# Moving half of the scores of squares of 16 to GpSimd and the gate's remainders to TensorE and ScalarE, in a four-layer hybrid kernel

## The chip, the cores and the metric

The kernel runs on one core of one Trainium2 chip. The metric is the device time of one execution in microseconds (us). The engines are called by the names that the profile uses: PE (TensorE, matrix products), PEld (its weight loads), DVE (VectorE), ACT (ScalarE), POOL (GpSimd) and SP (SyncE, which only issues transfers here). Each engine runs its own instructions strictly in the order in which they were written, and waits on semaphores for the others.

## The reference

Eight batches of 512 tokens of width 256 go through four residual layers, each on the layer-normed input: attention A, feed-forward, attention B, feed-forward.

```
Q, K, V = heads of x@Wq*C**-0.5, x@Wk, x@Wv     # 16 heads, C = 64
scores  = einsum('bshq,bshk->bshqk', Q, K)      # per token and head: 64 x 64
w       = softmax(scores masked to k <= q)
attn    = einsum('bshqk,bshk->bshq', w, V)
x = x + attn @ Wo                               # attention A

h = silu(x@w1 * s1) * (x@w2 * s2)               # the gate, 1024 wide
h = gelu(h@h1 * s);  h = gelu(h@h2 * s)         # two hidden layers
x = x + (h@w3) * s3                             # feed-forward
```

Attention A isn't attention over tokens. For every token and head it forms the outer product of the 64 query and 64 key entries, takes a causal softmax over it, and weighs the value entries. It has no matrix product in its core, so the work is elementwise, on DVE, ACT and POOL. Attention B is ordinary causal attention over the tokens, with 16 heads of 16.

## The kernel before

**Attention A.** The lower triangle of each 64 x 64 square is cut into squares: one of 32 x 32, two of 16 x 16, four of 8 x 8 and so on for each head, and the diagonal. A group is one tile of 128 tokens and four heads (256 columns); there are 8 x 4 x 4 = 128 groups. The work of a group is split into four units (line 553): unit 0 is the squares of 32 of two heads, unit 1 all squares of 16, unit 2 the squares of 32 of the other two heads, unit 3 the small squares. A unit goes through these stages, some steps apart:

- `scores` (line 784): the products of queries and keys, in pieces of 128 x 1024 elements. Units 0 and 2 run on POOL, two pieces each; units 1 and 3 on DVE, unit 1 in two pieces. POOL takes the query from an SBUF copy, DVE from PSUM.
- `exps` (line 798): the exponential, on ACT.
- `weigh` (line 808): times the values, on DVE.
- `halve` (line 814): one half of a unit's columns is added onto the other by a transfer that POOL issues.
- `fold` (line 819): for the squares of 32, POOL adds the two halves of what is left.
- `gather` (line 845): DVE sums over columns, into a small tile `red`.
- `add_rows` (line 852): POOL adds `red` to the group's accumulator. Then `invert` (line 856, DVE) and `divide` (line 860, POOL).

`AttentionA.step(n)` writes one step: unit n is scored, unit n-1 goes through the exponential, unit n-2 is weighed and halved, units n-3 to n-5 are folded and gathered. A step has three parts, set off by `yield`. The second part begins with the scores of units 1 and 3; then come the adds of the sums that were gathered before, the division, the small squares (lines 835 and 852) and the folds. The tile of unit 1 (`w16`) has one buffer, that of units 0 and 2 three.

**The rest.** Feed-forward and attention B of a batch are written as one generator, `after_a`, and are woven between the parts of attention A's steps. Each `yield` of the generator gives a number; the main loop draws from it until the sum of these numbers reaches `total` times the share of the batch's 64 steps that attention A has done. So the yields and `total` (line 1339) together set how far apart pieces of the feed-forward are written. Work of the other batch lags attention A by 75 steps: attention A runs alone at first, and the last batch's other layers run alone at the end.

**The gate.** Products are taken in fp32r, one pass each, so what comes out of the gate is kept as a high and a low part. For each of the eight chunks of 128 x 512 of a feed-forward: PE makes two products into two PSUM tiles; ACT takes silu of the first (line 1028); DVE multiplies by the second (line 1031); ACT rounds the result to fp32r (line 1035), the high part; POOL subtracts that from the result (line 1036), the low part. Each of these is written with `later`, and `flush` writes what is pending, so every chunk goes one stage further with each flush. The five buffers of PSUM pool `ps_f` rotate over all of this work. `plus` (line 472) adds a tile to a PSUM tile by a product with the identity. The hidden layers' products are line 1120, their gelus lines 1085 and 1087, their weights come by transfers which POOL issues (line 934). The feed-forward's last product is line 1146, attention B's are lines 1167 to 1276.

## Time and profile before

| what | value |
|---|---|
| time of three runs | 4002.61, 4003.38, 4004.08 us, median 4003.38 |
| the profiled execution | 4009.55 us, its span 4007.6 us |
| mean granted clock of PE | 0.845 |
| line 784 on POOL, 128 x 1024 | 512 instructions, mean 2102 ns |
| line 784 on DVE, squares of 16, 128 x 1024 | 256 instructions, mean 1219 ns |
| line 852 on POOL, sums of 32, 128 x 128 | 256 instructions, mean 701 ns |
| line 852 on POOL, sums of 16, 8 and 4, 128 x 256 | 384 instructions, mean 759 ns |
| line 819 on POOL, folds, 128 x 1024 | 256 instructions, mean 2512 ns |
| line 1036 on POOL, the gate's low part, 128 x 512 | 128 instructions, mean 1448 ns |
| line 1035 on ACT, the gate's high part, 128 x 512 | 128 instructions, mean 615 ns |

The profile shows one execution. Its span runs from the first to the last instruction; the execution's own time is a little longer. The mean of a group of instructions includes an overlap: where instructions follow each other without a gap, the distance from start to start is shorter than the mean, by 0.1 to 0.3 us. Busy shares are of the span, and an engine can be busy at its share and still wait for another once in each round.

### The profile page before, as it was taken

Reading aid. Unit: us, or ns where it says so; the run is one execution under the profiler, and the core shown is the slowest. Engines: PE = TensorE matmul, PEld = TensorE weight load, DVE = VectorE, ACT = ScalarE, POOL = GpSimd, SP = SyncE. Lnnn points to the kernel's source line nnn. Section 1 sums busy time; section 2 is a strip of 40 time slices with the busy share of each in tenths; the row PEclk is TensorE's granted clock in tenths of the full one; section 3 lists DMA queues with packets and bytes.
Section 4 is the critical chain, followed back from the end, with each engine's and each line's share of the span. In section 5 each row is a group of like instructions: output and inputs, shape, how many; then the busy total and the mean of one; then the engine's idle time right before and its main releaser. Section 6 shows DMA issues by size and latency. Waiting matters only on the chain.

```text
span 4007.6 us, 37678 instructions
## 1 busy us (share of the span) xinstructions
PE 2958.0 (74%) x12328; PEld 2012.2 (50%) x12328; DVE 3376.7 (84%) x3777; ACT 2337.2 (58%) x3145; POOL 3098.1 (77%) x3051
## 2 busy tenths in 40 slices
PE   1543478777876888768787788768787778768988
PEld 0311145355653656346553566346653556436847
DVE  4899988998889888998989988998889988897115
ACT  2433465666755766666755767567656667555342
POOL 6688888887888887887888888888888878886211
PEclk7555689888987989889897889879898899879999
DMA  8566777668776777668776688668877687767304
GB/s 240 114 141 145 146 182 182 147 161 199 199 162 126 195 188 196 150 147 210 174 192 139 168 198 214 147 131 198 195 181 151 154 199 205 155 133 210 126 29 167
DMA packets 118653, 671.07 MB, mean 167 GB/s; under 512 B 12704, under 2 KB 31915, under 8 KB 43824
## 3 DMA queue, kind: packets, MB, share of 16 engines
q0 software_dynamic: 78336, 570.46, 62.9%
q1 hardware_dynamic: 40112, 98.11, 6.8%
q8 instruction: 100, 1.64, 0.2%
q14 instruction: 105, 0.86, 0.1%
HBM read 255.90 MB, written 9.96 MB: 66 GB/s over the span
## 4 chain that ended last, share of the span: by engine, by line
DVE 38%; PE 16%; POOL 14%; DMA 12%; issue 8%; ACT 8%; POOLq 0%; DVEq 0%; ACTq 0%
DVE red L845 15%; DMA w<-w 12%; DVE w L808 10%; PE ph L1120 5%; ACT w L798 3%; POOL w L819 3%; DVE ws L808 3%; POOL w L784 3%; PE pqkb L1167 3%; DVE ws L784 3%; POOL acc L852 3%; DVE w L784 2%; POOL w L814 2%; DVE acc L856 2%; POOL h L1036 2%
## 5 line engine op out<-in xcount | busy, mean ns | idle before, releaser
L798 ACT ACTIVATE w<-w 128x2048 f32<-128x2048 f32 x384 | 734.2, 1913 | 653.8 <-POOL w L784 440.8
L1120 PE MATMUL ph<-h,hidden 128*128 128x512 f32 x4096 | 1047.9, 412 | 77.4 <-POOL h L1036 45.5
L784 POOL TENSOR_TENSOR w<-k 128x1024 f32<-128x1024 f32 x512 | 1076.2, 2102 | 9.6 <-ACT k L762 9.0
L1120 PEld LDWEIGHTS ph<-h,hidden 128*128 128x128 f32 x4096 | 795.3, 196 | 282.1 <-POOL h L1036 55.9
L808 DVE TENSOR_TENSOR w<-w,qv 128x1024 f32<-128x1024 f32 x768 | 899.8, 1213 | 22.4 <-ACT w L798 22.3
L845 DVE TENSOR_REDUCE red<-w 128x128 f32<-128x1024 f32 (+1 forms) x384 | 601.8, 1567 | 171.6 <-DMA w<-w 94.6
L819 POOL TENSOR_TENSOR w<-w 128x1024 f32<-128x1024 f32 x256 | 643.1, 2512 | 72.5 <-DMA w<-w 71.9
L814 POOL DMA_DIRECT2D w<-w x384 | 337.1, 878 | 339.7 <-issue 134.8
L852 POOL TENSOR_TENSOR acc<-acc,red 128x256 f32<-128x256 f32 (+1 forms) x640 | 471.0, 736 | 152.3 <-DVE red L845 124.5
L845 DVE TENSOR_REDUCE red<-ws 128x256 f32<-128x2048 f32 (+1 forms) x256 | 435.5, 1743 | 0.0
L746 PE MATMUL qv<-wqv,xnta 128*128 128x512 f32 x512 | 299.3, 715 | 89.9 <-DVE ws L808 82.4
L808 DVE TENSOR_TENSOR ws<-ws,qv 128x1024 f32<-128x1024 f32 (+3 forms) x512 | 294.7, 638 | 49.4 <-ACT ws L798 49.4
L1052 PE MATMUL pw<-xnt,gate 128*128 128x512 f32 (+2 forms) x1152 | 298.8, 419 | 24.9 <-ACT silu L1028 18.0
L784 DVE TENSOR_TENSOR w<-qv,k 128x1024 f32<-128x1024 f32 x256 | 301.3, 1219 | 3.6
L784 DVE TENSOR_TENSOR ws<-qv,k 128x1024 f32<-128x1024 f32 (+3 forms) x512 | 299.8, 648 | 0.0
L868 PE MATMUL bank<-ident,acc 128*128 128x128 f32 x256 | 64.3, 341 | 287.5 <-ACT k L761 287.1
L798 ACT ACTIVATE ws<-ws 128x1920 f32<-128x1920 f32 x128 | 231.5, 1809 | 75.3 <-DVE ws L784 74.7
L1052 PEld LDWEIGHTS pw<-xnt,gate 128*128 128x128 f32 x1152 | 227.6, 213 | 82.1 <-ACT silu L1028 22.3
L1229 ACT ACTIVATE eb<-psb 128x256 f32<-128x256 f32 (+3 forms) x512 | 182.2, 443 | 146.6 <-PE psb L1226 146.3
L1146 PE MATMUL pof<-w,h 128*128 128x256 f32 x1024 | 247.9, 396 | 19.4 <-ACT h L1085 19.4
L1085 ACT ACTIVATE h<-ph,s_sb 128x512 fp32r<-128x512 f32 (+1 forms) x256 | 171.1, 688 | 145.9 <-PE ph L1120 144.6
L856 DVE RECIPROCAL acc<-acc 128x256 f32<-128x256 f32 x128 | 223.2, 1744 | 12.3 <-POOL acc L852 12.3
(143 smaller groups left out, 4723.5 us busy)
## 6 DMA issues: line engine op xcount, KB each, us to landing
w<-w POOLq DMA_DIRECT2D x384, 1024.0 KB, 7.7
hidden<-in_h POOLq DMA_DIRECT2D x128, 1024.0 KB, 7.9
gate<-in_w12p POOLq DMA_DIRECT2D x32, 1024.0 KB, 9.0
w<-w_d SPq DMA_DIRECT2D x16, 1024.0 KB, 12.0
wqv<-wqv_d SPq DMA_DIRECT2D x31, 512.0 KB
wo<-in_wo SPq DMA_DIRECT2D x32, 256.0 KB, 7.4
wbqk<-wbqk_d SPq DMA_DIRECT2D x8, 1024.0 KB
w<-in_h SPq DMA_DIRECT2D x8, 1024.0 KB, 7.0
```

The lines of the kernel that those rows point to most:

```text
L746: nc.tensor.matmul(qv.rearrange("p j f -> p (j f)"), xnt[:, c, :], wqv[:, c, :], start=(c == 0), stop=(c == DC - 1),)
L784: eng.tensor_tensor(e, rows(q).to_broadcast(shape), columns(kt[:, 0]).to_broadcast(shape), ALU.mult)
L798: nc.scalar.activation(e, e, AF.Exp, scale=C**-0.5)
L808: nc.vector.tensor_tensor(ev, e, columns(qv[:, 1]).to_broadcast(list(e.shape)), ALU.mult)
L814: nc.gpsimd.dma_start(w[:, :2048], w[:, 2048:], accum_op=ALU.add)
L819: nc.gpsimd.tensor_tensor(w[:, :1024], w[:, :1024], w[:, 1024:2048], ALU.add)
L845: nc.vector.tensor_reduce(red, self.columns_of(w, n, off, nsq), AX.X, ALU.add)
L852: nc.gpsimd.tensor_tensor(rows, rows, part.rearrange("p a (x i) -> p a x i", i=n), ALU.add)
L856: nc.vector.reciprocal(acc[:, 0, :], acc[:, 0, :])
L1052: nc.tensor.matmul(pj[:, toks], w[:, m % 4, j, c, :], xs[:, p, c, toks], start=(p == 0 and c == 0), stop=(p == 1 and c == DC - 1),)
L1120: nc.tensor.matmul(pss[j], w[:, j, c, :], h_in(p, c), start=(p == 0 and c == 0), stop=(p == 1 and c == MC - 1),)
L1146: nc.tensor.matmul(po, h(0, c)[:, i * P : (i + 1) * P], w3[:, c, :], start=(c == 0), stop=False)
```

## The change

Four things are edited, and the pacing is adapted to them.

- Scores: the first of the two pieces of the squares of 16 is computed on POOL; the second stays on DVE. It is written where unit 1 was written before, at the start of the second part of its step.
- Sums of 32: units 0 and 2 write their sums into the two halves of one tile, which has one buffer, and POOL adds both to the accumulator at once, after unit 2. The tiles for 16, 8 and 4 have two buffers in place of three.
- Gate: in place of POOL's subtraction, PE makes the difference in PSUM, by a product of the identity with the result and one of the negative identity (`minus`, a new constant) with the high part, and ACT copies that into the low part. This is one stage more.
- Pacing: the gate flushes after each of its two products, not after both; its yields grow by 1.0 or 1.1 per chunk and there are three closing flushes in place of two; `total` goes from 309.5 to 328.9.

```diff
+    minus = const.tile([P, P], F32R, name="minus")
+    nc.scalar.activation(minus, ident, AF.Copy, scale=-1.0)
...
-            eng, q = (nc.gpsimd, kt[:, 1]) if n_u in (0, 2) else (nc.vector, qv[:, 0])
             for n, off, nsq, cols in squares(units[n_u]):
-                for e, ev, rows, columns in pieces(w, n, off, nsq, cols):
+                for p, (e, ev, rows, columns) in enumerate(pieces(w, n, off, nsq, cols)):
+
+                    on_pool = n == 32 or n == 16 and p == 0
+                    eng, q = (nc.gpsimd, kt[:, 1]) if on_pool else (nc.vector, qv[:, 0])
                     shape = list(e.shape)
                     eng.tensor_tensor(
...
                 if n > 2:
-                    red = ap_.tile([P, 2, nsq * n], F32, tag=f"red{nsq * n}", name=f"red_{b}_{i}_{g}_{n_u}_{n}", bufs=2 + (n < 32))
-                    nc.vector.tensor_reduce(red, self.columns_of(w, n, off, nsq), AX.X, ALU.add)
-                    self.sums.append((b, i, g, n, cols, red))
+                    if n_u != 2:
+                        red = ap_.tile(
+                            [P, 2, GW // 2], F32, tag=f"red{n // 32}", name=f"red{n}_{b}_{i}_{g}", bufs=1 + (n < 32)
+                        )
+                        self.live["red", n] = red
+                    red = self.live["red", n]
+                    part = red[:, :, cols.start // 2 : cols.stop // 2]
+                    nc.vector.tensor_reduce(part, self.columns_of(w, n, off, nsq), AX.X, ALU.add)
+                    if n_u != 0:
+                        self.sums.append((b, i, g, n, slice(0, GW), red))
...
             def high():
                 nc.scalar.copy(h(0, m), x)
-                later(lambda: nc.gpsimd.tensor_tensor(h(1, m), x, h(0, m), ALU.subtract))
+                later(low)
+
+            def low():
+                rest = ps_f.tile([P, S], F32, tag="pf", name=f"rest_{u}_{m}")
+                nc.tensor.matmul(rest, ident, x, start=True, stop=False)
+                nc.tensor.matmul(rest, minus, h(0, m), start=False, stop=True)
+                later(lambda: nc.scalar.copy(h(1, m), rest))
...
                 for j in range(2):
                     products(p[j], m, j, last if ps[0] else slice(0, S))
-                flush()
+                    flush()
                 later(lambda m=m, p=p, h=h: gate(m, *p, h))
-                yield 0.5 if ps[0] else 1.8
-        for _ in range(2):
+                yield 1.5 if ps[0] else 2.9
+        for _ in range(3):
             flush()
             yield 1
...
-    total = 309.5
+    total = 328.9
```

## The prediction

> **What bounds the kernel now.** I read the busy shares of the engines first, then the same shares by stretch of the span, then the timelines of GpSimd and VectorE in one quiet stretch, then the table of waits.
>
> ```profile
> PE 2958.0 (74%) x12328; PEld 2012.2 (50%) x12328; DVE 3376.7 (84%) x3777; ACT 2337.2 (58%) x3145; POOL 3098.1 (77%) x3051
> ```
>
> ```profile
> 200.00:600.00 400.00, 191.47 (x464) 107.26 (x463) 386.09 (x412) 181.55 (x197) 347.05 (x320) 0.62 0.71 153
> ...
> 1800.00:2200.00 400.00, 317.33 (x1359) 215.24 (x1359) 358.83 (x392) 257.33 (x345) 330.93 (x317) 0.89 0.76 180
> ...
> 3700.00:3800.00 100.00, 97.72 (x430) 80.63 (x429) 13.86 (x22) 33.68 (x57) 20.09 (x33) 0.98 0.40 132
> ```
>
> The columns of a stretch are its ends and length, then busy time of PE, weight loads, DVE, ACT and POOL. There are three regimes. Up to the first silu at 532 us the first attention runs alone and DVE is busy 386 of 400 us. From there to 3690 us feed-forward and second attention run between its steps, and DVE falls to 359 of 400 with POOL at 331: neither is full. In the last 317 us PE alone is busy.
>
> In the quiet regime a group (four units, one pass over 256 columns) takes 23.72 us: the chain of waits has its three reductions at 153.65, 177.37, 201.09 us and so on. One group on POOL, then on DVE (start, length, [idle before]):
>
> ```profile
> 255.77 0.87 POOL L814 DMA_DIRECT2D w<-w  x1 [2.66 <-issue]
> 256.38 2.35 POOL L852 TENSOR_TENSOR acc<-acc,red 128x128 f32<-128x128 f32 x3
> ...
> 263.79 2.62 POOL L819 TENSOR_TENSOR w<-w 128x1024 f32<-128x1024 f32 x1
> 266.29 0.81 POOL L852 TENSOR_TENSOR acc<-acc,red 128x256 f32<-128x256 f32 x1
> ...
> 269.36 2.36 POOL L819 TENSOR_TENSOR w<-w 128x1024 f32<-128x1024 f32 x1
> 271.68 1.95 POOL L784 TENSOR_TENSOR w<-k 128x1024 f32<-128x1024 f32 x1
> ...
> 263.86 2.28 DVE L845 TENSOR_REDUCE red<-w 128x256 f32<-128x2048 f32 x1
> 266.18 2.36 DVE L784 TENSOR_TENSOR w<-qv,k 128x1024 f32<-128x1024 f32 x2
> ...
> 272.17 1.22 DVE L845 TENSOR_REDUCE red<-w 128x128 f32<-128x1024 f32 x1
> ```
>
> DVE never stops. POOL's only pause is 2.66 us, before it issues the halving transfer of the squares of 16 (line 814), which waits for DVE's weighing. From there POOL runs without a gap to the second fold (line 819), which ends at about 271.70, and DVE needs that fold at 272.17. So POOL is 0.47 us from setting the pace, whatever its share of 77% says. The loop through both engines is: transfer issue to end of fold on POOL, 271.70 - 255.77 = 15.93; the reductions and the weighing on DVE up to the next issue, 1.13 + 3.32 + 2.26 = 6.71 by start-to-start times; 0.6 for two handovers (weighing ends 255.23, issue 255.77). That is 23.25, beside DVE's own 23.72.
>
> ```profile
> DVE silu L1031 <- ACT silu L1028: 55.0, 28, 5.0
> ...
> PE ph L1120 <- POOL h L1036: 45.5, 26, 6.0
> ...
> ACT silu L1028 <- POOL h L1036: 43.0, 30, 3.5
> ```
>
> The columns are total us, times and longest. These waits are the gate's: POOL's subtraction (line 1036) holds the next silu, and that holds DVE and PE.
>
> **What the Trainium skill says.** "GPSIMD Engine Reference", section 3.1, has two-input elementwise work about 1.96 times slower on GpSimd than on VectorE; here the same 1024 elements of line 784 take 2102 ns against 1219, a ratio of 1.72. "Perfetto Trace Analysis", section Identifying the Most-Contended Engine, would have the fullest engine relieved first; that engine is DVE, and the change does it, but the loop above is one that shares of busy time don't show. "PSUM — Partial Sum Buffer" says that GpSimd cannot touch PSUM; the code agrees, for the POOL piece takes its query from the SBUF copy kt[:, 1].
>
> **The change part by part.**
>
> *Squares of 16.* DVE loses one of two pieces a group: 266.18 + 2.36 for two, start to start 2.27, so 1.13 each. POOL gains one piece at 1.92 (start to start, from 250.46 to 252.38; the nearest rows bound it: DVE's own 1.13, and 2.32 for POOL's fold of the same size, which would make the loop 0.4 longer, some 25 us over the kernel's tight groups). It stands in the second part of step 1, ahead of the add of the previous group's sums of 16, the small squares and the second fold. Its tile w16 has one buffer, so it waits for DVE's reduction of the previous group, which ends at 266.14; POOL comes free at 266.29, so the wait costs nothing now. But everything queued behind is 1.92 late, the second fold first; DVE's reduction of it waits, and behind that on DVE stand 3.32 us of reductions and the weighing that the next transfer waits for. The exponential of this unit has 6 us of room (ends 270.53, used at about 276.6), so it isn't late.
>
> *Sums of 32.* Two adds of 128x128 become one of 128x256 at about the same price (rows of 701 and 759 ns), so one of 0.73 goes from POOL. It stood at 252.38, straight before the 2.66 us pause, so the loop gains nothing; if the pause were gone it would be worth 0.73 x 128 = 93 us. The DVE reductions stay. The buffers (one for 32, two for the rest) are written 6 or more us after the adds that free them: nothing.
>
> Quiet regime: DVE alone would need 23.72 - 1.13 = 22.59; the loop needs 23.25 + 1.92 = 25.17. Period up by 1.45. From 142 to 532 us there are 390 / 23.72 = 16.4 groups: **+24 us**.
>
> *The same in the middle regime.* For each of its 109 groups I took from the timeline by how much DVE arrives after the second fold's end. If the room is r, the change is 1.92 - r, but not below -1.13. By classes: 37 groups with r near 0.49 (most of second attention): +53. 26 with r about 1.72: +5. 20 with r over 2.2 (mean 5.2, around the gates): -23. 9 where DVE already waits for POOL's fold: +17. 17 where the fold itself waits some 4 us for its transfer, in which the new piece is hidden: at best -1.13 or a little less, -14 together. Sum **+38 us**. PE also works harder per step here, as the pacing total goes from 309.5 to 328.9, so other stages pass in 6% fewer steps; the -23 and -14 may not be had, so this term is +35 to +75.
>
> *Gate.* Off POOL: 128 subtractions, 1.3 us each start to start, 166 us in all, some 8 in each of 16 stages. On PE: an fp32 identity product of 512 columns and an fp32r one. The tail gives 16 fp32 products of 256 columns in 3.45 us, so 0.43 for 512; and 256 fp32r ones in 58.03, so 0.23. 0.66 x 128 = 84 us, hidden in the middle regime (317 of 400 busy). On ACT: a copy of 0.61, 78 us. The yields stretch the stage from 2 x 1.4 + 2 x 0.5 + 6 x 1.8 + 2 = 16.6 units of pacing to 2.8 + 2 x 1.5 + 6 x 2.9 + 3 = 26.2; a batch has 64 steps of three parts, so that is 16.6 / (309.5 / 192) = 10.3 parts against 26.2 / (328.9 / 192) = 15.3, 3.4 steps to 5.1. ACT loads a table (1283 ns) for silu and again for exp in each step with a gate; 1.7 steps more make 3 to 4 loads, 4 to 5 us a stage, and with the copies (8 x 0.61 = 4.9) some 9 us. In 1456 to 1491 us ACT is already busy 29.8 of 35, so per group it will stand near 32: it becomes the stage's limit at a pace close to today's. "ScalarE: Activation LUTs", section What ACT_TABLE_LOAD costs, has the same 1283 ns and a drain of about 1380 besides; in this trace an exponential starts 1.3 us after its load, so I don't add the drain. PSUM rotates 5 buffers over three tiles per chunk in place of two: nothing while the yields keep chunks 4 us apart. Gain bounded above by the DVE idle before line 1031 (67 us) and as much again in PE's waits and the catch-up after; below by 5 us lost in each of 14 stages (-70 of gain). I take a small gain, 10 us: **-10**.
>
> *Tail.* Two gate stages on PE alone: 16.32 us for 64 products now, plus 8 x 0.66 = 5.3. Waiting by the PSUM rotation for copy, high part, silu and product in a row (0.61 + 0.61 + 0.69 + 0.75 and handovers, 3.0 per chunk against 2.7 of PE) adds up to 2.4 each. 10.6 to 18: **+14**. The constant and its one ACT pass: under 1.
>
> Sum: 24 + 38 - 10 + 14 = **+66 us**. On the profiled execution's span of 4007.6 (own time 4009.55) that gives 4073.6; its own time stands 6.2 above the median of 4003.38. 4003.4 + 66 = **4069 us**.
>
> **Rivals.** *The gates win, and the kernel is faster.* If taking 166 us from POOL lets the gate groups run like their neighbours: the timeline has about 67 us for the two groups around a gate, and 2 x 28 for two DVE-bound ones with feed-forward work. 11 x 14 = 154: 24 + 38 - 154 + 14 = -78, 3925 us. It decides from (24 + 38 + 14) / 14 = 5.4 us a stage. For it: the three waits shown. Against: ACT's load of 29.8 in 35 us, which grows. *ACT or PSUM chokes the gate.* 5 us lost per stage: 24 + 38 + 70 + 14 = +146, 4149. For it: two engines more in the chain, and PE now waits in order for ACT's high part. Against: slower pacing. *No change*: the fold's delay is absorbed by rooms that I counted as tight, 4003. Against: a 23.72 us period with DVE full and 0.47 of room.
>
> **How the numbers follow.** Forecast 0.66 (own range 4015 to 4125), gates win 0.13, choked gate 0.17, no change 0.04. Under 0.2%, 8 us, a run of this kernel can't tell from nothing: faster is the second case, same the fourth, slower the other two, 0.83. The range 4000 to 4140 leaves out most of the 0.13 and the upper third of the 0.17.
>
> **What would show it.** In the quiet regime the period becomes 25.2 and DVE waits 2.5 us for the second fold; if it falls to 22.6, the loop is wrong. Waits for line 819 on DVE rise from 77 us to some 150 or more. The gate stages show more silu table loads than 49, no wait for POOL, and PE waits for ACT. The last 317 us become about 331. The forecast is wrong if the gate stages gain over 5 us each, or if the rooms of the middle regime aren't those of before, since every group's alignment shifts.

## The result, and the profile after

The changed kernel takes **4200.98 us** (median of four runs, 4194.04 to 4204.81) against 4003.73 for the kernel before on the same chip: a ratio of **1.0483**, interval 1.0457 to 1.0509. The forecast was 4069 us, 4000 to 4140. The direction was right; the loss is 197 us where 66 were booked, and lies outside the range.

The experiments below ran on chips where the kernel before took 4010 to 4014 us, so kernels are compared by ratios, and phases by the spans of profiled executions. The span of the changed kernel is 4192.3 us (its own time 4194.04), 184.7 more than before. To place the difference I cut each span at the reciprocals of the 128 groups (line 856 before, 867 after): the start up to the first one, the first 16 groups, six batches of 16 groups, the last 15, and what follows the last. The period in quiet is the mean of eight intervals, from the third on.

| kernel | span | start | first 16 groups | one batch, mean of six | last 15 | tail | period in quiet |
|---|---|---|---|---|---|---|---|
| before | 4007.6 | 86.2 | 413.1 | 461.2 | 421.6 | 319.2 | 23.72 |
| after | 4192.3 | 92.7 | 433.2 | 480.1 | 445.3 | 340.3 | 25.47 |
| scores alone | 4166.4 | 92.5 | 431.6 | 479.8 | 441.4 | 322.0 | 25.23 |
| gate and pacing alone | 4081.2 | 84.1 | 409.8 | 470.1 | 428.9 | 337.8 | 23.72 |
| sums of 32 alone | 3993.0 | 84.6 | 412.8 | 459.0 | 421.1 | 320.5 | 23.72 |

So the 184.7 are 6.5 at the start, 20.1 in the quiet groups, 6 x 18.9 = 113 in the batches, 23.7 in the last 15 groups and 21.1 in the tail. The quiet part was forecast well. Most of the miss is in the middle, 137 us with the last 15 groups, where 28 were booked (38 for the scores less 10 for the gate).

The engines' shares of the page after, and then three stretches, the first two at the same times as before, the third in this kernel's tail (columns: ends, length, busy time and count of PE, weight loads, DVE, ACT, POOL, then PE's clock, the DMA share and GB/s; here DVE and POOL are read):

```profile
PE 3065.8 (73%) x12712; PEld 2053.6 (49%) x12712; DVE 3241.0 (77%) x3649; ACT 2462.1 (59%) x3318; POOL 3157.2 (75%) x2923
```

```profile
200.00:600.00 400.00, 170.96 (x370) 87.61 (x369) 352.70 (x376) 169.73 (x186) 349.25 (x296) 0.59 0.66 140
1800.00:2200.00 400.00, 319.70 (x1279) 229.00 (x1279) 325.29 (x371) 268.16 (x339) 321.24 (x304) 0.89 0.72 173
3900.00:4000.00 100.00, 97.53 (x409) 76.74 (x408) 12.82 (x24) 33.30 (x58) 10.16 (x25) 0.98 0.34 111
```

DVE fell from 84% to 77%, POOL from 77% to 75%. Every elementwise engine that was near its limit became emptier, and the kernel slower. In 1800 to 2200 us DVE fell from 359 of 400 to 325 and POOL from 331 to 321, so nothing became full there. The quiet group on POOL, then on DVE (start, length, idle before it):

```profile
302.81 2.21 POOL L788 TENSOR_TENSOR w<-k 128x1024 f32<-128x1024 f32 x1
304.72 0.97 POOL L863 TENSOR_TENSOR acc<-acc,red 128x256 f32<-128x256 f32 x1
...
307.95 2.34 POOL L823 TENSOR_TENSOR w<-w 128x1024 f32<-128x1024 f32 x1
...
317.67 0.87 POOL L818 DMA_DIRECT2D w<-w  x1 [2.70 <-DVE w L812]
318.28 2.62 POOL L863 TENSOR_TENSOR acc<-acc,red 128x256 f32<-128x256 f32 x3
...
305.19 2.34 DVE L812 TENSOR_TENSOR w<-w,qv 128x1024 f32<-128x1024 f32 x2
310.33 1.22 DVE L855 TENSOR_REDUCE red<-w 128x128 f32<-128x1024 f32 x1 [2.80 <-POOL w L823]
```

The new piece of line 788 stands ahead of the adds and of the second fold (307.95), and DVE now waits 2.80 us for that fold. POOL in turn waits 2.70 us for DVE's weighing. The loop through both engines is the pace, as forecast. Two rows of the table of waits before, and then the table after (total us, times, longest):

```profile
POOL acc L852 <- DVE red L845: 124.5, 57, 23.4
...
DVE red L845 <- POOL w L819: 76.9, 30, 5.6
```

```profile
ACT w L802 <- POOL w L788: 745.3, 213, 13.1
DVE red L855 <- POOL w L823: 298.2, 112, 7.5
...
POOL w L788 <- DVE red L855: 139.9, 61, 20.7
...
DVE silu L1042 <- ACT silu L1039: 125.7, 75, 3.7
...
PEld rest L1052 <- ACT h L1046: 55.3, 50, 3.3
```

DVE's wait for the fold rose from 76.9 to 298.2 us, and its wait for silu from 55.0 to 125.7. The third line is new: the score piece on POOL waits for DVE's reduction of the group before. POOL waited for that reduction before as well, 124.5 us, but at the add behind the place where the piece now stands. The first line is less new than it looks. ACT's idle time before its exponentials of units 0 to 2 (line 798 before, 802 after) is 654 us before and 747 after; before the change 186.3 us of it stood under DVE, which computed both pieces of unit 1.

### The profile page after: what moved, and what is told of

Read it like the earlier page. It is cut to its first block, busy times and chain, and to the rows that moved or that the text cites. A ratio compares the mean times of both kernels' runs of the same rounds, so it can differ in the third digit from the quotient of the medians.

```text
span 4192.3 us, 38393 instructions
## 1 busy us (share of the span) xinstructions
PE 3065.8 (73%) x12712; PEld 2053.6 (49%) x12712; DVE 3241.0 (77%) x3649; ACT 2462.1 (59%) x3318; POOL 3157.2 (75%) x2923
## 5 line engine op out<-in xcount | busy, mean ns | idle before, releaser
L788 POOL TENSOR_TENSOR w<-k 128x1024 f32<-128x1024 f32 x640 | 1339.3, 2093 | 150.3 <-DVE red L855 139.9
L1137 PE MATMUL ph<-h,hidden 128*128 128x512 f32 x4096 | 1010.4, 403 | 17.0 <-DMA hidden<-in_h 13.0
L855 DVE TENSOR_REDUCE red<-w 128x128 f32<-128x1024 f32 (+1 forms) x384 | 602.2, 1568 | 376.3 <-POOL w L823 298.2
L1137 PEld LDWEIGHTS ph<-h,hidden 128*128 128x128 f32 x4096 | 775.1, 191 | 206.4 <-issue 20.7
L863 POOL TENSOR_TENSOR acc<-acc,red 128x256 f32<-128x256 f32 x512 | 421.0, 822 | 26.2 <-DVE red L855 6.3
L1069 PE MATMUL pw<-xnt,gate 128*128 128x512 f32 (+2 forms) x1152 | 305.0, 416 | 26.5 <-DVE xnt L994 14.2
L812 DVE TENSOR_TENSOR ws<-ws,qv 128x1024 f32<-128x1024 f32 (+3 forms) x512 | 295.0, 637 | 35.1 <-ACT ws L802 34.6
L1069 PEld LDWEIGHTS pw<-xnt,gate 128*128 128x128 f32 x1152 | 223.6, 209 | 91.9 <-DVE xnt L994 18.6
L743 PE MATMUL bank<-wk,xnta 128*128 128x256 f32 x512 | 158.0, 437 | 121.8 <-ACT x L898 117.2
L1163 PEld LDWEIGHTS pof<-w,h 128*128 128x128 f32 x1024 | 200.4, 198 | 69.3 <-ACT h L1102 35.2
```

The source lines that it names most:

```text
L788: eng.tensor_tensor(e, rows(q).to_broadcast(shape), columns(kt[:, 0]).to_broadcast(shape), ALU.mult)
L812: nc.vector.tensor_tensor(ev, e, columns(qv[:, 1]).to_broadcast(list(e.shape)), ALU.mult)
L855: nc.vector.tensor_reduce(part, self.columns_of(w, n, off, nsq), AX.X, ALU.add)
L863: nc.gpsimd.tensor_tensor(rows, rows, part.rearrange("p a (x i) -> p a x i", i=n), ALU.add)
L1069: nc.tensor.matmul(pj[:, toks], w[:, m % 4, j, c, :], xs[:, p, c, toks], start=(p == 0 and c == 0), stop=(p == 1 and c == DC - 1),)
L1137: nc.tensor.matmul(pss[j], w[:, j, c, :], h_in(p, c), start=(p == 0 and c == 0), stop=(p == 1 and c == MC - 1),)
```

## The experiments

My theory after the result was that the scores cost nearly all of it, through POOL's queue; its rivals were the gate with its pacing, and ACT's exponential, which now waits for POOL. A batch's 16 groups are called places 0 to 15.

### The three parts, each alone

**Scores alone:**

```diff
-            eng, q = (nc.gpsimd, kt[:, 1]) if n_u in (0, 2) else (nc.vector, qv[:, 0])
...
+                    on_pool = n == 32 or n == 16 and p == 0
+                    eng, q = (nc.gpsimd, kt[:, 1]) if on_pool else (nc.vector, qv[:, 0])
```

> Only the first part: the first piece of the squares of 16 goes to GpSimd; sums, gate and pacing as before. Both theories expect the quiet stretch at 25.2 us a group (23.72 before; 25.5 with the whole change) and some 6 us at the start. Queue theory (the layer norm's small operations stand longer in GpSimd's queue, and that is what stretches the handovers at the end of second attention and of feed-forward): the group at the end of second attention takes 40 us or more as with the whole change (33.4 before), and the total is 4130 to 4180 us. Pacing theory (the handovers are stretched because the new yields weave the pieces at other places): those groups stay within 2 us of before, and the total is 4050 to 4090 us.

Measured: ratio 1.0379 (1.0358 to 1.0399). In the quiet stretch 25.23 us a group, where the loop gave 25.17. The total is what the queue theory expected, but not the group at the end of second attention: it takes 35.3 us, not 40.

**Gate and pacing alone** (the constant `minus`, and the edits of the pacing, which are shown two runs below, besides this):

```diff
-                later(lambda: nc.gpsimd.tensor_tensor(h(1, m), x, h(0, m), ALU.subtract))
+                later(low)
+
+            def low():
+                rest = ps_f.tile([P, S], F32, tag="pf", name=f"rest_{u}_{m}")
+                nc.tensor.matmul(rest, ident, x, start=True, stop=False)
+                nc.tensor.matmul(rest, minus, h(0, m), start=False, stop=True)
+                later(lambda: nc.scalar.copy(h(1, m), rest))
```

> Only the gate's remainders by TensorE and ScalarE with the new pacing; scores and sums as before. Quiet stretch unchanged at 23.7 us a group; the stretch after the first attention's end longer by about 20 us, as with the whole change. Pacing theory: the stretched handovers are here too, 4100 to 4130 us. Queue theory: they are not, and the gate's own relief of GpSimd shows: 4000 to 4030 us.

Measured: ratio 1.0177 (1.0154 to 1.0200). It loses 8.9 us a batch and 18.6 in the tail. The total, 4084 us, is what neither theory expected.

**Sums of 32 alone:**

```diff
-                    self.sums.append((b, i, g, n, cols, red))
...
+                    part = red[:, :, cols.start // 2 : cols.stop // 2]
+                    nc.vector.tensor_reduce(part, self.columns_of(w, n, off, nsq), AX.X, ALU.add)
+                    if n_u != 0:
+                        self.sums.append((b, i, g, n, slice(0, GW), red))
```

> Only the row sums of the squares of 32 added together. One add less in a pause of GpSimd, but one of the three adds that stand in the loop grows from 0.73 to about 1.0 us: the loop goes from 23.25 to some 23.5 us and stays under VectorE's 23.72. Quiet stretch unchanged. Forecast of both theories: 4003 us, plus or minus 10.

Measured: ratio **0.9946** (0.9927 to 0.9966), a little faster than both kernels. The quiet period stays at 23.72, so the loop gains nothing, as forecast; the gain is 2.2 us a batch in the middle, where POOL's queue is one add shorter. That the shorter queue is its cause isn't shown: in two other kernels below the same edit is worth 0.1% and 0.3%.

**Pacing alone** (POOL still subtracts):

```diff
-                flush()
+                    flush()
                 later(lambda m=m, p=p, h=h: gate(m, *p, h))
-                yield 0.5 if ps[0] else 1.8
-        for _ in range(2):
+                yield 1.5 if ps[0] else 2.9
+        for _ in range(3):
...
-    total = 309.5
+    total = 328.9
```

> Only the pacing: a flush after each product, yields larger by 1.0 or 1.1 a chunk, three closing flushes, total 328.9; GpSimd still subtracts. Pacing theory: the group at the end of second attention is stretched to about 40 us and the total is 4080 to 4120 us. Queue theory: no stretched handover, and the gate spread out over more steps lets GpSimd's subtractions interfere less: 3980 to 4010 us.

Measured: ratio 1.0134 (1.0112 to 1.0156), 7.7 us a batch. The total, 4067 us, lies below the pacing theory's range, but the group at the end of second attention takes 40.5 us, as it expected. So the pacing, for which the forecast had no term of its own, costs three quarters of what the gate part costs. The three parts multiply to 1.0379 x 1.0177 x 0.9946 = 1.0506, against 1.0483 for all together, so over the whole time they nearly add up. In the middle they don't: by the spans of the table the parts lose 131 + 61 - 14 = 178 us in the batches and the last 15 groups, all together 137. Each span is one execution, and these stand up to 7 us off their kernels' medians, so a part of the difference may be that; the rest means that what the scores and the pacing cost there overlaps. The shares below are those of each part alone.

### Why the scores cost so much

**An extra piece.** GpSimd computes the piece in addition to VectorE, into a place of the same tile that VectorE then overwrites. VectorE is relieved of nothing. The exponential should not have depended on POOL here, but the trace shows that it does.

```diff
+                    if n == 16 and eng is nc.vector and not self.extra:
+                        self.extra = True
+                        nc.gpsimd.tensor_tensor(
+                            ev, rows(kt[:, 1]).to_broadcast(shape), columns(kt[:, 0]).to_broadcast(shape), ALU.mult
+                        )
                     eng.tensor_tensor(
```

> The kernel before with one piece of work added: GpSimd computes the first piece of the squares of 16 a second time, where e1_scores computes it, into a place that VectorE overwrites two steps later. VectorE still computes both pieces, so no exponential waits for GpSimd. Both theories expect the quiet stretch at 25.2 us a group, since the second fold is as late as in e1_scores. Queue theory (the 18.6 us a batch that e1_scores loses come from GpSimd's queue and the fold behind the piece): 15 us a batch or more are lost here too, a ratio of 1.033 or more. Exponential theory (they come from ScalarE, which stands waiting for GpSimd's piece and holds the feed-forward's work behind it; that wait rose from 441 to 790 us): 8 us a batch or less, a ratio of 1.015 to 1.025.

Measured: ratio 1.0388 (1.0371 to 1.0405), and 25.24, 479.8 and 441.7 us in the three phases, where scores alone has 25.23, 479.8 and 441.4. The two kernels can't be told apart: the means of each of a batch's 16 places agree within 0.7 us. The table of waits has a row that was meant to be absent:

```profile
ACT w L804 <- POOL w L786: 70.4, 21, 12.7
```

In none of the 128 groups does the exponential of the squares of 16 start before the extra piece (line 786) has ended. ACT's idle time before the exponentials of units 0 to 2 is 790 us here and 792 with the scores alone, and before those of unit 1 alone 268 with the extra piece, 247 with the scores alone, 212 before. So the pair tests little but DVE's 1.13 us less per group, which is worth nothing that can be measured. It doesn't test the exponential. The loss comes with the piece on POOL: from what stands behind it in POOL's queue, from what the piece waits for, or from what waits for it.

**The extra piece set aside.** The third line of the waits above leaves a doubt. The piece is written into the tile of the squares of 16, which has one buffer, so it waits for DVE's reduction of the group before; the forecast had priced this wait at nothing. In this kernel the extra piece goes into a bfloat16 tile of its own that nothing reads; to make room, the small tiles `red` have two buffers each. The exponential is free of the piece too: it starts before the piece's end in 15 groups, and ACT's idle time before it is 210 us, as before.

```diff
+                        aside = wt.tile([P, 1024], BF16, tag="aside", name=f"aside_{b}_{i}_{g}").rearrange(
+                            "p (a r) -> p a r", a=shape[1]
+                        )
                         nc.gpsimd.tensor_tensor(
-                            ev, rows(kt[:, 1]).to_broadcast(shape), columns(kt[:, 0]).to_broadcast(shape), ALU.mult
+                            aside, rows(kt[:, 1]).to_broadcast(shape), columns(kt[:, 0]).to_broadcast(shape), ALU.mult
```

> The kernel before, in which GpSimd computes the first piece of the squares of 16 a second time as in the kernel with the extra piece, but writes it into a small bfloat16 tile of its own that nobody reads, so that the piece doesn't wait for VectorE's reduction of the group before (the tile of the squares of 16 has one buffer, and in the kernel with the extra piece GpSimd waits 137 us for that reduction in 55 places, just ahead of the piece). Three small result tiles have two buffers in place of three, to make room. It separates the load from the wait. Theory one, the load alone: the piece costs the same wherever its result goes, the ratio stays at 1.039 within 0.003. Theory two, the wait: in the quiet stretch, where GpSimd isn't waiting at that place, a group still takes 25.2 us, but in the 55 places the piece fits into the wait that the add behind it has anyway, so some 50 x 1.9 = 95 us of the 155 come back, and the ratio is 1.012 to 1.022.

Measured: ratio 1.0278 (1.0258 to 1.0299), between the two theories. The quiet period is 25.21; a batch takes 473.9 us in place of 479.8, the last 15 groups 435.3 in place of 441.7. POOL's timeline with the extra piece, in a group with feed-forward work:

```profile
1910.46 2.61 POOL L825 TENSOR_TENSOR w<-w 128x1024 f32<-128x1024 f32 x1
1914.46 1.96 POOL L786 TENSOR_TENSOR w<-k 128x1024 f32<-128x1024 f32 x1 [1.39 <-DVE red L851]
1916.37 0.74 POOL L858 TENSOR_TENSOR acc<-acc,red 128x256 f32<-128x256 f32 x1
...
1919.39 2.38 POOL L825 TENSOR_TENSOR w<-w 128x1024 f32<-128x1024 f32 x1
```

and with the piece set aside:

```profile
1894.63 2.63 POOL L828 TENSOR_TENSOR w<-w 128x1024 f32<-128x1024 f32 x1
1896.96 2.20 POOL L789 TENSOR_TENSOR aside<-k 128x1024 bf16<-128x1024 f32 x1
1900.08 0.74 POOL L861 TENSOR_TENSOR acc<-acc,red 128x256 f32<-128x256 f32 x1 [0.92 <-DVE red L854]
...
1903.11 2.36 POOL L828 TENSOR_TENSOR w<-w 128x1024 f32<-128x1024 f32 x1
```

In the first the piece stops for DVE's reduction and then runs, and everything behind it comes after. In the second it runs while POOL would wait for that same reduction anyway, since the add behind it needs the sum. From the first fold to the second it is 8.93 us against 8.48 here. The rows of POOL's wait for that reduction, with the extra piece and with it set aside:

```profile
POOL w L786 <- DVE red L851: 137.3, 55, 23.0
```

```profile
POOL acc L861 <- DVE red L854: 52.6, 25, 20.8
```

Over the span, sharing the tile costs 4165.8 - 4125.5 = 40 us; the plain load of 1.92 us a group is the rest, 118 us. The 40 us take in both waits, the piece's for the reduction and the exponential's for the piece, and no run separates them. Of the 41 us in the 112 groups from the 17th on, 30 fall in the 54 groups in which the piece waited for the reduction (39 or 16, if the interval before or after a group's own is taken), which speaks for the first.

To see where, I sorted the 112 groups from the 17th on by the forecast's rule, by the profile of before, and added up how much longer the interval ending at each group became. The counts come out at 37, 24, 20, 9 and 22; the forecast had 37, 26, 20, 9 and 17, since short waits for a transfer are counted here too.

| groups, by the room of before | booked | scores alone | extra piece | set aside |
|---|---|---|---|---|
| room about 0.5 us | +53 | +57.5 | +56.7 | +48.4 |
| room about 1.7 us | +5 | +11.1 | +12.8 | +3.7 |
| wide room, around the gates | -23 | +36.8 | +37.0 | +27.5 |
| DVE waits for the fold already | +17 | +9.0 | +9.3 | +11.9 |
| the fold waits for its transfer | -14 | +18.3 | +16.8 | -0.2 |
| sum | +38 | +132.7 | +132.6 | +91.3 |

The split is rough, since a delay can show an interval earlier or later: with the interval before a group's own, the scores alone give +47.5 for the small rooms and +32.5 for the wide ones, with the one after it +40.1 and +38.9. With its own, the small rooms come out as forecast. Wherever one cuts, the wide rooms lose where gains were booked. For the two rows with booked gains, 37 together, there is a loss of 53.8 with the extra piece, of which the shared tile explains 26.5.

**The piece later.** POOL takes the second piece in place of the first, and writes it after the folds:

```diff
-                for _ in self.scores(*unit):
-                    pass
+                half = self.scores(*unit)
+                next(half)
+                if unit[3] == 3:
+                    for _ in half:
+                        pass
...
                 self.fold(b, i, g, u)
+            if unit[3] == 1:
+                for _ in half:
+                    pass
...
-                    on_pool = n == 32 or n == 16 and p == 0
+                    on_pool = n == 32 or n == 16 and p == 1
```

> Only the scores on GpSimd, as in e1_scores, with one difference: GpSimd's piece of the squares of 16 is written after the folds of its step, and VectorE's piece first. The same instructions on the same engines; nothing waits behind the new piece that VectorE needs soon. Loop theory (the piece costs because it stands ahead of the second fold): the quiet stretch falls to 23.3 us a group (25.23 in e1_scores, 23.72 before), and most of the loss of 18.6 us a batch goes too: a ratio of 0.995 to 1.005. Load theory (1.9 us more per group on GpSimd stretch the groups in which it also serves the feed-forward, wherever the piece stands): the quiet stretch falls to 23.3, but each batch still loses 10 us or more: a ratio of 1.015 or more.

Measured: ratio 1.0599 (1.0581 to 1.0617). The quiet period falls from 25.23 to 24.14, not to the expected 23.3, and a batch takes 496.2 us. The same with the sums of 32:

> e5_late and the sums of the squares of 32 added together. Quiet stretch 23.5 us (the add in the loop is 0.28 longer). Sums alone gave a ratio of 0.9946; if it helps by taking 0.7 us a group from GpSimd it should help here more: 0.5 to 1% below e5_late.

Measured: ratio 1.0584 (1.0566 to 1.0601), 0.1% below, where 0.5 to 1% was expected. Its table of waits begins:

```profile
ACT w L806 <- POOL w L792: 901.5, 200, 18.0
PE bank L883 <- ACT k L767: 820.8, 119, 13.0
```

The fold is in time now, but ACT, working in order, stands at the late exponential, and with it what is behind it: the copies from PSUM into `k`, for which PE's next product into that bank waits (820.8 us, before 287.1). So in this kernel I moved the exponential of unit 1 by one part as well:

```diff
-            if self.at(n - 1)[0] is not None:
-                self.exps(*self.at(n - 1))
+            scored = self.at(n - 1)
+            if scored[0] is not None and scored[3] != 1:
+                self.exps(*scored)
...
                 self.project(b, i, g)
+            if scored[3] == 1:
+                self.exps(*scored)
```

> e6_late_sums with the exponential of the squares of 16 written one part later, at the end of the second part of its step, so that ScalarE does what is ready before it waits for GpSimd's late piece. If ScalarE's standing before that exponential is what made e5_late and e6_late_sums lose 34 us a batch, most of it comes back: quiet stretch 23.3 to 23.8 us, 465 us a batch or less, a ratio of 0.99 to 1.01. If the load on GpSimd itself costs, a batch stays at 480 us or more, a ratio of 1.03 or more.

Measured: ratio 1.0307 (1.0290 to 1.0324); a batch takes 478.0 us in place of 494.9. The expectation of 0.99 to 1.01 missed. Where the exponential stands is worth half of the loss of a batch. Its wait isn't gone, though; what it holds up is another copy:

```profile
ACT w L809 <- POOL w L795: 855.1, 243, 17.4
...
PE bank L894 <- ACT att L728: 285.6, 60, 9.4
...
PE bank L886 <- ACT k L770: 60.9, 38, 5.1
```

PE's wait for the copies into `k` is 60.9 us in place of 820.8, but that for the copy into `att` 285.6, where it was 17.9 in the kernel before this one. So the 17 us a batch that are left can't be put down to the load on POOL alone.

### Pacing and its alignment

In the pacing kernel two of a batch's 16 groups are much longer: place 6, at the start of attention B (27.5 to 33.4 us), and place 11, at its end (33.5 to 40.5), where the layer norm of the second feed-forward is computed and also the statistics of the next batch for attention A. In the whole change they take 33.4 and 42.0 us. Place 11 of the whole change, on DVE, ACT and POOL:

```profile
2299.57 0.18 DVE L527 BATCH_NORM_AGGREGATE mv<-st 128x2 f32<-128x6 f32 x1
2309.46 0.42 DVE L994 TENSOR_TENSOR xnt<-ps_ln,xnt 128x256 fp32r<-128x256 f32 x1 [9.70 <-ACT xnt L987]
2309.80 1.21 DVE L855 TENSOR_REDUCE red<-w 128x128 f32<-128x1024 f32 x1
...
2308.02 0.60 ACT L540 ACTIVATE xn<-x,shift,rstd 128x256 f32<-128x256 f32 x1 [7.80 <-POOL shift L534]
...
2309.04 0.38 ACT L987 CAST xnt<-ps_ln 128x256 fp32r<-128x256 f32 x1
...
2299.56 1.94 POOL L788 TENSOR_TENSOR w<-k 128x1024 f32<-128x1024 f32 x1
2301.45 0.95 POOL L818 DMA_DIRECT2D w<-w  x1
2302.14 2.26 POOL L788 TENSOR_TENSOR w<-k 128x1024 f32<-128x1024 f32 x1
2304.49 0.23 POOL L531 TENSOR_SCALAR rstd<-mv 128x4 f32<-128x4 f32 x1
...
2307.76 0.23 POOL L534 TENSOR_SCALAR shift<-shift 128x1 f32<-128x1 f32 x1
```

Read it backwards. DVE's reduction of attention A stands behind the low part of a normed tile (line 994), which waits 9.70 us for ACT's cast. The cast stands on ACT behind the normalising of another tile, which waits 7.80 us for its scale. And POOL computes the scale only after two score pieces, a transfer and another set of statistics, those of the next batch (128 x 4). DVE's part of attention A stands still for some 10 us, and DVE and ACT both have work queued behind their waits. At the corresponding place before and with the pacing alone, on DVE:

```profile
2221.13 0.42 DVE L983 TENSOR_TENSOR xnt<-ps_ln,xnt 128x256 fp32r<-128x256 f32 x1 [1.12 <-ACT xnt L976]
```

```profile
2242.54 0.42 DVE L983 TENSOR_TENSOR xnt<-ps_ln,xnt 128x256 fp32r<-128x256 f32 x1 [6.75 <-ACT xnt L976]
2242.88 1.21 DVE L845 TENSOR_REDUCE red<-w 128x128 f32<-128x1024 f32 x1
```

If this is a matter of how the two streams are aligned, a shift of the whole second stream should mend it. Pacing alone, one step later, then one part later:

```diff
-                while 3 * spent * each < total * (3 * (n - each - 11) + part + 1):
+                while 3 * spent * each < total * (3 * (n - each - 12) + part + 1):
```

> The pacing alone, as in e4_pacing, with the other layers written one step later against the first attention (75 steps of lag become 76). Alignment theory (the two handovers stretched by the pacing, 40.5 and 33.4 us, are so because their layer norm now falls on a bad place of a step of the first attention): another place, so these groups change by 3 us or more, and the ratio leaves 1.0134 by 0.5% or more. Rate theory (the slower gate and the 6% faster remainder cost by themselves): these groups stay within 1 us, and the total moves by under 8 us.

Measured: ratio 1.0040 (1.0028 to 1.0053).

```diff
-                while 3 * spent * each < total * (3 * (n - each - 11) + part + 1):
+                while 3 * spent * each < total * (3 * (n - each - 11) + part):
```

> As e7_lag12, but later by one part of a step, a third of it, in place of a whole step. Alignment theory: the stretched handovers change by 3 us or more, in either direction. Rate theory: within 1 us of e4_pacing.

Measured: ratio 1.0047 (1.0030 to 1.0064). Each shift takes back most of 1.34%: a batch falls from 468.9 to 462.4 and 463.2 us, where it takes 461.2 before. Place 11 falls from 40.5 to 34.1 and 34.6 us. Place 6 falls to 30.7 with the first shift, but rises to 36.3 with the second. The whole change, one part later:

> The whole change with the other layers written one part of a step later, as in e8_part1. If alignment acts in the whole change as in the pacing alone, the handover of 42 us falls to about 36 and the ratio from 1.0483 to 1.038 to 1.044. If the handovers of the whole change are GpSimd's queue, the ratio stays within 0.4% of 1.0483.

Measured: ratio 1.0402 (1.0385 to 1.0419), where the change has 1.0483. Place 11 falls from 42.0 to 36.0, place 6 rises to 36.6. And the kernel before, one part later:

> The kernel before with nothing changed but the other layers written one part of a step later. If the place of the handovers in a step of the first attention is worth what the pacing runs say, single groups move by 3 us or more and the total by more than its 0.2%, either way; if the kernel before is insensitive, a ratio of 0.998 to 1.003.

Measured: ratio 1.0057 (1.0040 to 1.0073). So the alignment that the kernel before has is better than the one beside it, and in these three kernels a shift of a third of a step is worth half a per cent or more, up or down.

### The gate

**Gate with the old pacing** (`minus` and `low` as above, and one closing flush more):

```diff
-        for _ in range(2):
+        for _ in range(3):
```

> The gate's remainders by TensorE and ScalarE with the old flushes, yields and total, and only the third closing flush that the longer chain needs. The tail is 20 us longer as with the whole change. If taking 166 us from GpSimd is worth something in the 14 gates that run beside the first attention, it shows here, with nothing of the pacing in it: 3 us a gate would be 42 us, a ratio of 0.995. If ScalarE is the gate's limit instead, the gates take as long as before or longer: a ratio of 1.005 or more.

Measured: ratio 1.0094 (1.0077 to 1.0111). A batch takes 462.1 us, 0.9 more than before, and the tail 353.9, 35 more; I put that down to the third flush's yield, which `total` doesn't count here, so that more work is left for the end. The ratio lies where the theory of ACT as the limit had it, but 35 of the 44 us by which the span grows are the tail's. So exchanging 128 subtractions on POOL for products and copies gains nothing in the middle. What the relief of POOL is worth alone this doesn't show: the products and copies cost something too, and the third flush shifts the streams against each other, by which other kernels gained or lost more than the 0.9. DVE's wait for silu is 97 us, before 55.

**The subtraction on DVE:**

```diff
-                later(lambda: nc.gpsimd.tensor_tensor(h(1, m), x, h(0, m), ALU.subtract))
+                later(lambda: nc.vector.tensor_tensor(h(1, m), x, h(0, m), ALU.subtract))
```

> The kernel before with one operation moved: the gate's subtraction on VectorE in place of GpSimd, 128 of about 0.7 us; pacing, flushes and stages as before. Theory that the gain of the gate's relief was eaten by what replaced it (a copy on ScalarE, two products that wait for ScalarE, one stage more): here none of that is, and the groups around the gate fall by 2 us or more each, a batch by 4 us or more, a ratio of 0.985 to 0.993. Theory that GpSimd's subtractions were not what the gate waited for: the batch stays within 2 us, a ratio of 0.998 to 1.005.

Measured: ratio 1.0056 (1.0039 to 1.0072), which neither theory had. Busy time in one group with a gate, place 1 of a batch, before:

```profile
1918.90:1952.40 33.50, 26.31 (x97) 18.90 (x96) 28.89 (x34) 28.34 (x34) 28.02 (x26) 0.90 0.65 153
```

and with the subtraction on DVE:

```profile
1921.40:1958.00 36.60, 28.47 (x99) 19.34 (x97) 36.60 (x40) 29.05 (x34) 23.43 (x20) 0.91 0.61 143
```

Before, DVE, ACT and POOL are all busy 28 to 29 of 33.5 us. With the subtraction on DVE, DVE is busy the whole 36.6. Part of that is subtractions that last longer: most take 0.68 us, but 35 of 128 take over 0.9, and the longest 2.84; why isn't shown. So no engine has much room in a gate group. With the sums of 32 besides:

> e13_gate_vector and the sums of the squares of 32 added together (e3_sums: 0.9946). Both take work from GpSimd alone, so the gains should add: 0.5% below e13_gate_vector. If either theory of e13_gate_vector holds, this is also the version to beat both kernels.

Measured: ratio 1.0028 (1.0017 to 1.0039), 0.3% below in place of 0.5, and not faster than the kernel before.

## Why the prediction was right and wrong

**Quiet regime, +24: right.** The period was forecast at 25.17 and is 25.23 with the scores alone, DVE's wait for the fold at 2.5 and is 2.80. The whole change has 25.47, because the wide add of the sums of 32 stands inside the loop, after the transfer: the three adds take 2.58 us from start to start after, 2.30 before. Over the stretch that the forecast took, from 142 to 532 us before, the change loses 25.6 us and the scores alone 21.8; the 20.1 of the table's first 16 groups take in a first interval that became shorter. The start, which I didn't book, lost 6.5 more.

**Middle regime, +38: the step that failed.** The scores alone cost 131 us there (6 x 18.6 in the batches and 19.8 in the last 15 groups). Three terms were wrong.
- "Its tile w16 has one buffer ... so the wait costs nothing now" was read off one quiet group. There it holds: 25.21 us without that wait, 25.24 with it. In the groups with other work it does cost: with the extra piece POOL waits 137 us in 55 places, 54 of them there, and sharing the tile costs 40 us of span, in which the exponential's wait for the piece is contained.
- "1.92 - r, but not below -1.13" credits DVE with what it is relieved of. The extra piece relieves it of nothing and takes the same time in every phase: no credit can be measured, and the -37 go. The Trainium skill's page "Perfetto Trace Analysis", section Identifying the Most-Contended Engine, would relieve the fullest engine first; here that is DVE, and its relief alone is worth less than can be measured (1.0379 with it, 1.0388 without).
- The wide rooms didn't absorb the load. With the piece set aside, the 20 groups still lose 27.5 us, 1.4 each. The room was read as slack on DVE. In 10 of the 20 groups DVE came late because it was itself waiting, for silu between its two reductions, and silu waits for POOL: ACT's wait for POOL's subtraction is 43.0 us before, 67.3 with the piece set aside, 77.5 with the scores alone, and DVE's wait for silu rises from 55.0 to 79.0 with the piece set aside. That a piece in POOL's queue delays both ends of the measured room is what these waits suggest for these 10. In the other 10 DVE had products of the gate or statistics to do and didn't wait, and they lose as much, 18.3 against 18.4 us with the scores alone. So silu's wait isn't the whole of it; no run isolated a cause, and it stays open.

**Pacing: a term that was missing.** "Other stages pass in 6% fewer steps", with the middle at +35 to +75, was as near as I came. Alone it costs 54 us by its ratio. Most of that is alignment, at the layer norm of place 11 above all, and not the density of PE's work: one step's or one part's shift leaves the density as it is and takes back most.

**Gate, -10: wrong in sign.** The term took in the stretched stage; gate and pacing together cost 61 us in the middle (6 x 8.9 and 7.3), most of it the pacing. The gate's own part is small: with the old pacing a batch loses 0.9 us, and with the new one 1.2 (470.1 against 468.9). That ACT would load more tables was right: silu's loads go from 49 to 72. But that is the pacing, which alone has 72, while the gate with the old pacing has 50. DVE's wait for silu is 88.3 us with the pacing alone and 125.7 in the whole change; that waits for POOL are exchanged for waits for ACT and PE is seen in the 55.3 us in which PE's weight loads wait for the high part.

**Tail, +14: measured 21.** I had 0.66 us for the two products of a remainder. The tail on PE:

```profile
3900.46 2.00 PE L1069 MATMUL pw<-xnt,gate 128*128 128x512 f32 x8
...
3902.30 1.02 PE L1051 MATMUL rest<-silu,ident 128*128 128x512 f32 x2
3902.76 0.79 PE L1052 MATMUL rest<-h,minus 128*128 128x512 f32 x1
3903.39 2.00 PE L1069 MATMUL pw<-xnt,gate 128*128 128x512 f32 x8
```

From 3902.30 to 3903.39 they take 1.09 us. A chunk takes 2.93 us (3900.46 to 3903.39) where it took 2.04, and PE runs through: the wait by PSUM's rotation, up to 2.4 a stage, isn't there. 16 chunks by 0.89 are 14 of the 21 us; the rest I didn't trace.

**Sums of 32, nothing: wrong by 0.5%.** The loop has nothing from it, as I said. But I had priced a shorter queue by the quiet loop alone; what it is worth in the middle differs from kernel to kernel.

**The exponential "isn't late": nearly so.** ACT's idle time before the exponentials of the squares of 16 is 212 us before, 247 with the scores alone and 204 in the whole change. What the 35 us of the scores alone cost no run shows. In the kernel with the piece after the folds the same exponential is late and does cost.

**Rivals.** The choked gate (4149) came nearest in time, by another cause: the gate's own part is about 1 us a batch. Gates that win didn't come: with 128 fewer subtractions on POOL a batch gains nothing, whether PE and ACT or DVE do the work in its place. No change is excluded by the quiet period, 25.47 in place of 23.72.

## What to carry to other kernels

In a pipeline of engines that work in order and wait for each other, the price of an operation depends on its place in a queue, and the engine's share doesn't tell it: 1.92 us on a POOL that was 77% busy cost 1.2 us a group, and 1.13 us taken from a DVE that was 84% busy brought nothing that could be measured. Room at a wait isn't slack by itself: 20 groups with over 2.2 us of it lost 37 us to a piece of 1.92, and what makes the other side late may come from the engine that gets the work. A buffer that costs no wait in one stage has to be priced in each of the others. Woven streams have an alignment, which was worth half a per cent or more in each of the three kernels shifted by a part: when a part is re-paced, compare it at several shifts before judging what it does.

## What the runs showed of the hardware

- An fp32 product with the identity of 512 columns appears as two instructions in the records (256 for 128 products in the changed kernel, line 1051; the fp32r product of line 1052 as one), and the pair takes 1.09 us from start to start; from other rows of the trace I had 0.66.
- A multiply of 1024 elements on POOL takes 1.91 us from start to start whether it writes fp32 or bfloat16 (304.49 to 306.40 us in the kernel with the piece set aside, 302.81 to 304.72 in the changed one).
